# Where the attention values stand around a loop of routed expert tiles, and how scores are masked

## The chip, the cores and the metric

The kernel runs on one core of one Trainium2 chip. The metric is the device time of one execution in microseconds (us); all times below are in us unless a line says ns. Engines are named as in the profile: PE is TensorE (PEld its weight loads), DVE the vector engine, ACT ScalarE, POOL GpSimd, SP the engine that issues most DMAs.

## The reference, cut to what matters

Two layers over x of shape 2048 x 512, each of the form `x + attention(norm(x)) * silu(ffn(norm(x)))`. The change lies in the second layer:

```python
# attention: 28 pooled keys (means over 64 tokens) for the first 1792 tokens, the last 256 tokens as keys of their own
scores = (q_sem @ k_sem2.T + q_geo @ k_geo2.T) / sqrt(32) * exp(logit_scale)   # 16 heads
scores = where(k_pos <= pos, scores, -1e9)
s = (softmax(scores) @ v2) @ Wo
# mixture of experts: 2 shared experts, and the 4 best of 16 routed ones for each token
ffn = u + shared(u) + sum_over_chosen(gate * (relu(u @ w1 + b1) @ w2 + b2))
x = x + s * silu(ffn)
```

A token at position p sees the pooled keys of blocks that end at or before p. The first 63 tokens see none; for them the softmax over equal scores is uniform over all keys, local ones included.

## The kernel before, in words

All arithmetic is float32. The 2048 tokens are 16 attention tiles of 128 rows (`NT`). Tiles 14 and 15 (`FULL`) also see local keys and are done early, in `full_group`, beside shared-expert matmuls. Tiles 0 to 13 see pooled keys only: tile i uses the first (i+1)*2 of them (tile 0 uses all 32 columns, because of its rows that see nothing). `KP` is 32 columns for the pooled keys, `NARROW` is 16. For tiles with at most 16 keys the scores lie in a `near` buffer, else in a `wide` one (three of each, taken in turn).

The work on a pair of tiles ("block" b of 256 tokens, seven in all) has three sorts of parts:

- `queries` (L1352 to L1368): two parts, each a projection `pq` of 16 matmul records on TensorE and four vector operations, with loads of cosines and sines;
- `scores` (L1560 to L1572, then `softmax`, L1325 to L1335): one part per tile, eight plus eight matmul records into `ps`, a product with the mask `m_pool`, the addition of `n_pool`, maximum, subtraction, Exp on ScalarE, sum, reciprocal, product;
- `values` (L1585 to L1597): one part per tile, transposes `pt`, a ScalarE copy to `sT`, matmuls `pw` with the values that are already folded with Wo, and a ScalarE copy into `xT`, which then holds the attention output of that tile.

A masked score is made as `score * 0 + (-1e9)`, an open one as `score * 1 + 0`; `m_pool` and `n_pool` hold the factors and addends for all 16 tiles (`NT`) side by side, `m_full` and `n_full` those of the full tiles. They are built on POOL at L765 to L792, ahead of the gathers of `yg` (L832).

The routed experts are a list of up to 80 tiles of 128 rows (`NRT`), of which at least 64 (`FULL_TILES`) are in use. `hidden_rows(j)` loads the weights and rows of tile j, transposes the rows (`tp`, L1678), and makes the hidden rows (`ph`, L1685; `ht`, L942). `down_rows` (`py`, L1709; `y`, L1714) makes the outputs of the tile before and adds them to the sums `comb` in DRAM by two indirect DMAs on POOL's queue (L1717). From j = 65 on, each step is inside a conditional `tc.If(held > j - 1)` (L1749), whose content is a unit of its own. Attention parts are put between the routed tiles: 30 of the 42 parts are spread over the first 64 steps, and the last 12 behind the conditional steps (`LATE`, `parts_by`, `attend_by`). These twelve are the queries of blocks 5 and 6, the scores of tiles 10 to 13 and the values of tiles 10 to 13.

Behind the loop the kernel closes: for each of eight pairs of attention tiles it loads the sums from `comb` (L1777), applies Silu on ScalarE (L1783), multiplies by `xT` (L1785), adds the residual `xo` (L1789) and stores the result (L1790).

The framework's planner orders the instructions of each engine at build time. It goes by program order, but moves work ahead that it takes for ready while an engine would be idle. `tc.keep_in_program_order(ins)` ties an instruction behind the one traced before it on its engine in the same block of code.

Of the kernel before, what the change touches and what calls it, by code (L numbers as in the profile page):

```python
# [9 lines left out]
F32 = mybir.dt.float32  # L10
# [67 lines left out]
def tile_kernel(ctx: ExitStack, tc: tile.TileContext, a: dict):  # L78
# [656 lines left out]

    sm_sem = ak.tile([P, HKV, 4], F32, name="sm_sem")
    sm_geo = ak.tile([P, 2, 8], F32, name="sm_geo")
    m_pool = ak.tile([P, NT, KP], F32, name="m_pool")
    n_pool = ak.tile([P, NT, KP], F32, name="n_pool")
    wt_pool = ak.tile([P, KP], F32, name="wt_pool")  # L740
    oh = ak.tile([P, NRT, NR], F32, name="oh")
# [22 lines left out]

    nc.gpsimd.memset(m_pool, 1.0)  # L765
    nc.gpsimd.memset(n_pool, 0.0)
    for t_, fill in ((m_pool, 0.0), (n_pool, MASKED)):
        nc.gpsimd.affine_select(
            out=t_, in_=t_, compare_op=ALU.is_ge, fill=fill, base=1 - MB,
            pattern=[[P, NT], [-MB, KP]], channel_multiplier=1,  # L770
        )
    nc.gpsimd.memset(m_pool[:, :, NBLK:KP], 0.0)
    nc.gpsimd.memset(n_pool[:, :, NBLK:KP], PADDED)


# [2 lines left out]
    nc.gpsimd.memset(wt_pool[:, NBLK : NBLK + 1], float(LW))  # L778


    m_full = ak.tile([P, KA], F32, name="m_full")
    n_full = [ak.tile([P, KP + (u + 1) * P], F32, name=f"n_full{u}") for u in range(len(FULL))]
    nc.gpsimd.memset(m_full, 1.0)
    for u, i in enumerate(FULL):
        nc.gpsimd.memset(n_full[u], 0.0)
        nc.gpsimd.tensor_copy(n_full[u][:, 0:KP], n_pool[:, i, :])
    for t_, fill in ((m_full, 0.0), *((t_, MASKED) for t_ in n_full)):
        own = t_[:, t_.shape[1] - P :]
        nc.gpsimd.affine_select(
            out=own, in_=own, compare_op=ALU.is_ge, fill=fill, base=0,  # L790
            pattern=[[-1, P]], channel_multiplier=1,
        )  # L792

# [525 lines left out]
    aps = ctx.enter_context(tc.tile_pool(name="aps", bufs=3, space=PSUM))  # L1319
    QB = 256  # L1320

    def softmax(s, heads, keys, neg, wt=None, last=True):

        sh_ = [P, heads, keys]
        nc.vector.tensor_tensor(out=s, in0=s, in1=bc(neg, 1, sh_), op=ALU.add)  # L1325
        mx = small.tile([P, heads], F32, tag=f"mx{heads}", name="mx")
        nc.vector.tensor_reduce(out=mx, in_=s, axis=AX.X, op=ALU.max)
        nc.vector.tensor_tensor(out=s, in0=s, in1=bc(mx, 2, sh_), op=ALU.subtract)
        nc.scalar.activation(s, s, AF.Exp)
        if wt is not None:  # L1330
            nc.vector.tensor_tensor(out=s, in0=s, in1=bc(wt, 1, sh_), op=ALU.mult)
        nc.vector.tensor_reduce(out=mx, in_=s, axis=AX.X, op=ALU.add)
        nc.vector.reciprocal(out=mx, in_=mx)
        if last:
            nc.vector.tensor_tensor(out=s, in0=s, in1=bc(mx, 2, sh_), op=ALU.mult)  # L1335
        return mx
# [39 lines left out]
    with tc.tile_pool(name="fw", bufs=1, side="right") as fw:  # L1376
# [51 lines left out]
        def full_group(u, g, woa):  # L1428
# [6 lines left out]
            for h in range(4):  # L1435
                rr = slice(HP * (h % 2), HP * (h % 2) + HP)
                ps = aps.tile([P, KA], F32, tag="pa", name="ps")
                nc.tensor.matmul(
                    out=ps[:, 0:nk], lhsT=qf[rr, 2 * g + h // 2, cols], rhs=kf[rr, g, 0:nk],
                    start=True, stop=True,  # L1440
                )
                nc.vector.tensor_tensor(
                    out=s[:, h, :], in0=ps[:, 0:nk], in1=m_full[:, KA - nk :], op=ALU.mult
                )
            mx = softmax(s, 4, nk, n_full[u], last=False)
            sp = fw.tile([P, 4, KP], F32, tag="sp", bufs=2, name="sp")
            for out, ks in ((sp, slice(0, KP)), (s[:, :, KP:nk], slice(KP, nk))):
                nc.vector.tensor_tensor(
# [91 lines left out]

    wide = [aq.tile([P, H, KP], F32, name=f"wide{i}") for i in range(3)]
    near = [aq.tile([P, H, NARROW], F32, name=f"near{i}") for i in range(3)]
    for t_ in (*wide, *near):
        nc.gpsimd.memset(t_, 0.0)
# [1 line left out]
    def room_of(i):  # L1548

        if i == 0:  # L1550
            return aq.tile([P, H, KP], F32, tag="t1", name="all_keys"), KP
        nk = (i + 1) * P // MB
        return (near if nk <= NARROW else wide)[i % 3], nk

    def scores(i, qg, u):
        cols = slice(u * P, (u + 1) * P)
        room, nk = room_of(i)
        ps = aps.tile([P, H, nk], F32, tag="pa", name="ps")
        for c in range(NC):
            nc.tensor.matmul(  # L1560
                out=ps, lhsT=xT[:, c, i * P : (i + 1) * P], rhs=sem[:, c, :, 0:nk],
                start=(c == 0), stop=False,
            )
        for p in range(2):
            for hf in range(2):
                nc.tensor.matmul(
                    out=ps[:, 8 * p : 8 * p + 8, :], lhsT=qg[:, p, hf, cols],
                    rhs=kd_geo[:, hf, 8 * p : 8 * p + 8, 0:nk], start=False,
                    stop=(p == 1 and hf == 1),
                )  # L1570
        s = room[:, :, 0:nk]
        nc.vector.tensor_tensor(  # L1572
            out=s, in0=ps, in1=bc(m_pool[:, i, 0:nk], 1, [P, H, nk]), op=ALU.mult
        )
        softmax(s, H, nk, n_pool[:, i, 0:nk], wt_pool if i == 0 else None)
        return room

    def values(i, s):
        keys = s.shape[2]
        each = P // keys  # L1580
        by_row = vo if keys == KP else vo8
        nw = H // each
        pt = aps.tile([P, nw, P], F32, tag="pa", name="pt")
        for g in range(nw):
            nc.tensor.transpose(  # L1585
                pt[:, g, :], s[:, each * g : each * (g + 1), :].rearrange("p h k -> p (h k)"),
                ident,
            )
        sT = aq2.tile([P, HKV, P], F32, tag="sT", name="sT")
        nc.scalar.copy(sT[:, 0:nw, :], pt)  # L1590
        pw = aps.tile([P, NC, P], F32, tag="pa", name="pw")
        for g in range(nw):
            nc.tensor.matmul(  # L1593
                out=pw.rearrange("p c t -> p (c t)"), lhsT=sT[:, g, :], rhs=by_row[:, g, :],
                start=(g == 0), stop=(g == nw - 1),
            )
        nc.scalar.copy(xT[:, :, i * P : (i + 1) * P], pw)  # L1597

    def attention():


        nb = FULL[0] * P // QB
        n = QB // P
        got = {}

        def start(b):
            return queries(
                b, aq, lambda shape: [aq.tile(shape, F32, tag=t, name=t) for t in ("t1", "t2")]
            )

        def score(b, u, q):
            got[b * n + u] = scores(b * n + u, q[0], u)

        def value(i):
            values(i, got.pop(i))

        for b in range(nb - 1):
            q = start(b)
            yield from q[1]
            if b < nb - 2:  # L1620
                for u in range(n):
                    score(b, u, q)
                    yield
                for u in range(n):
                    value(b * n + u)
                    yield
        assert n == 2
        for u in range(n):
            score(nb - 2, u, q)
            yield  # L1630
        q = start(nb - 1)
        yield from q[1]
        value((nb - 2) * n)
        yield
        for u in range(n):
            score(nb - 1, u, q)
            yield
        for i in ((nb - 2) * n + 1, (nb - 1) * n, (nb - 1) * n + 1):
            value(i)
            yield  # L1640


    iop = m1f.tile([P, 1], I32, name="iop")
# [76 lines left out]
            )  # L1720

    FULL_TILES = T * KR // P
    MAYBE = NRT - FULL_TILES
    PARTS = 6 * (FULL[0] * P // QB)
    LATE = 12
    attend = attention()
    rest_of = {}
    held = nc.values_load(
# [1 line left out]
        skip_runtime_bounds_check_because="it is a sum of counts, FULL_TILES to NRT",  # L1730
    )

    def parts_by(j):

        if j < FULL_TILES:
            return (j + 1) * (PARTS - LATE) // FULL_TILES
        return PARTS - LATE + (j - FULL_TILES) * LATE // MAYBE

    pending, taken = None, 0

    def attend_by(j):
        nonlocal taken
        while taken < parts_by(j):
            next(attend)
            taken += 1

    for j in range(NRT + 1):

        with contextlib.ExitStack() as more:  # L1749
            if j > FULL_TILES:  # L1750
                more.enter_context(tc.If(held > j - 1))
            made = hidden_rows(j) if j < NRT else None
            if j <= FULL_TILES:
                attend_by(j)
            if pending is not None:
                down_rows(*pending)
            pending = (j, *made) if made is not None else None
# [1 line left out]
            if 0 <= i < NT and i % 2 == 0:  # L1759
# [2 lines left out]
                    out=xo, in_=xr1[i * P : (i + 2) * P, :].rearrange("(n p) d -> p n d", p=P)  # L1762
                )
                rest_of[i] = xo
        if j > FULL_TILES:
            attend_by(j)
    assert next(attend, None) is None

    tiles.close()
# [4 lines left out]
    for i in range(0, NT, 2):  # L1774
# [4 lines left out]
                in_=c_[i * P : (i + 2) * P, :].rearrange("(n p) d -> p n d", p=P),  # L1779
            )  # L1780
        sums_of[i] = y
    for i, y in sums_of.items():
        nc.scalar.activation(y, y, AF.Silu)  # L1783
        y4 = y.rearrange("p n (c t) -> p n c t", t=P)
        nc.vector.tensor_tensor(  # L1785
            out=y4, in0=xT[:, :, i * P : (i + 2) * P].rearrange("p c (n t) -> p n c t", t=P),
            in1=y4, op=ALU.mult,
        )
        nc.vector.tensor_tensor(out=y, in0=y, in1=rest_of[i], op=ALU.add)  # L1789
        nc.sync.dma_start(  # L1790
            out=a["out"][i * P : (i + 2) * P, :].rearrange("(n p) d -> p n d", p=P), in_=y
        )


# [91 lines left out]
```

## Time and profile before

| what | before |
|---|---|
| runs | 1944.71, 1953.96, 1950.14; median 1950.14 |
| profiled execution: time, span | 1940.83, 1939.1 |
| TensorE busy, granted clock | 96% of the span, 0.986 |
| DVE, ACT, POOL busy | 41%, 27%, 24% |
| routed tiles run in the profiled execution | 74 with hidden rows, 73 with outputs |
| TensorE's work on the last routed tile ends | 1862.2 |
| last indirect add is issued | 1873.2 |
| first load of `comb` is issued | 1881.5 |

The profiled execution is one of the faster ones: its time lies 9.3 below the median. A row of a timeline gives start, duration, engine, line, operation, output and inputs, shape and count; in brackets stands how long the engine was idle before it and what ended that. TensorE's matmuls in float32 are recorded as two instructions each.

### The profile page before, as it was taken

What the parts mean: (1) busy time and instruction counts of PE and PEld (TensorE: products, weight loads), DVE (VectorE), ACT (ScalarE), POOL (GpSimd) and SP (SyncE); (2) the same over time, 40 slices, a digit from 0 to 9 for tenths busy, and PEclk for the clock granted to TensorE, in tenths of its full rate; (3) what the DMA queues carried; (4) which work ended last, traced back from release to release, by engine and by line L of the source; (5) the groups of instructions that cost most, each with busy time, mean ns of one, the idle gap of its engine ahead of it and who ended that gap; (6) DMA issues with size and microseconds to landing.
All of it is one profiled execution on the core that took longest, in us unless ns stands there. A gap on an engine that the chain in (4) does not pass through costs nothing.

```text
span 1939.1 us, 23212 instructions
## 1 busy us (share of the span) xinstructions
PE 1857.2 (96%) x8107; PEld 1292.1 (67%) x8107; DVE 787.3 (41%) x1565; ACT 532.9 (27%) x994; POOL 465.9 (24%) x350
## 2 busy tenths in 40 slices
PE   5899999999999999999989999999999999999977
PEld 4677777787877777777533654444767777777654
DVE  8713627272634545252166544331323232223116
ACT  6212322232323232232134212221222222222223
POOL 1301212121201111020210453000344444444430
PEclk9799999999999999999999999999999999999998
DMA  7548685635654443436461553022999999999963
GB/s 250 205 144 278 205 306 178 221 108 163 197 195 141 130 131 125 157 98 233 147 227 46 174 215 114 31 95 87 313 290 316 320 311 298 292 282 265 299 148 131
DMA packets 214096, 381.35 MB, mean 197 GB/s; under 512 B 16972, under 2 KB 134476, under 8 KB 213080
## 3 DMA queue, kind: packets, MB, share of 16 engines
q1 hardware_dynamic: 183896, 332.78, 50.7%
q0 software_dynamic: 28784, 45.63, 10.7%
q10 hardware_dynamic: 1296, 1.41, 0.3%
q8 instruction: 67, 1.10, 0.2%
q14 instruction: 53, 0.43, 0.1%
HBM read 294.04 MB, written 85.72 MB: 196 GB/s over the span
## 4 chain that ended last, share of the span: by engine, by line
PE 83%; DMA 6%; DVE 3%; issue 2%; POOL 2%; ACT 2%; SPq 0%; POOLq 0%; ACTq 0%; DVEq 0%
PE pg L571 23%; PE py L593 12%; PE ph L1685 9%; PE py L1709 9%; PE proj L416 7%; PE py L1105 4%; PE ph L956 3%; PE pw L1593 2%; DMA comb<-y,to 2%; PE pq L1352 2%; PE tp L1678 1%; PE po L712 1%; PE ps L1560 1%; PE pl L870 1%; PE pw L1477 1%
## 5 line engine op out<-in xcount | busy, mean ns | idle before, releaser
L571 PE MATMUL pg<-xg,w 128*128 128x256 f32 (+1 forms) x2304 | 497.8, 369 | 3.3 <-ACT xg L563 3.3
L571 PEld LDWEIGHTS pg<-xg,w 128*128 128x128 f32 x2304 | 420.9, 191 | 95.0 <-issue 42.1
L1717 POOL DMA_INDIRECT comb<-y,to x146 | 226.9, 1554 | 300.0 <-DMA comb<-y,to 222.2
L593 PE MATMUL py<-wd,hT 128*128 128x512 f32 x544 | 256.9, 593 | 2.9 <-DVE hT L578 2.9
L1685 PEld LDWEIGHTS ph<-xg,w 128*128 128x128 f32 (+1 forms) x1776 | 201.9, 182 | 39.8 <-ACT xg L1680 32.9
L1685 PE MATMUL ph<-xg,w 128*128 128x128 f32 (+1 forms) x1776 | 214.4, 277 | 1.5 <-DMA w<-in_w_dram 1.5
L1709 PE MATMUL py<-w,ht 128*128 128x512 f32 (+1 forms) x438 | 209.1, 593 | 0.0
L578 DVE TENSOR_TENSOR hT<-sg,pg 128x256 f32<-128x256 f32 (+1 forms) x144 | 57.0, 402 | 338.4 <-ACT sg L576 338.3
L576 ACT ACTIVATE sg<-pg 128x256 f32<-128x256 f32 (+1 forms) x144 | 53.5, 372 | 419.7 <-PE pg L571 419.4
L593 PEld LDWEIGHTS py<-wd,hT 128*128 128x128 f32 x544 | 102.1, 190 | 72.2 <-issue 61.9
L1714 DVE TENSOR_SCALAR y<-py,g 128x512 f32<-128x512 f32 x73 | 54.6, 749 | 206.7 <-PE py L1709 196.1
L942 ACT ACTIVATE ht<-ph,b1t 128x128 f32<-128x128 f32 (+1 forms) x222 | 81.3, 366 | 178.9 <-PE ph L1685 161.4
L1709 PEld LDWEIGHTS py<-w,ht 128*128 128x128 f32 (+1 forms) x438 | 75.1, 191 | 49.8 <-issue 49.3
L1680 ACT COPY xg<-tp 128x512 f32<-128x512 f32 x74 | 43.4, 586 | 177.2 <-PE tp L1678 166.4
L1105 PE MATMUL py<-w,hT 128*128 128x512 f32 (+1 forms) x192 | 89.3, 596 | 0.0
L956 PE MATMUL ph<-xT,w 128*128 128x512 f32 (+1 forms) x192 | 88.0, 597 | 0.0
L1043 POOL DMA_INDIRECT xs<-acc,slot x64 | 63.1, 985 | 67.2 <-DMA xs<-acc,slot 43.5
L1352 PE MATMUL pq<-xT,wqg 128*128 128x256 f32 x224 | 56.6, 401 | 14.2 <-DVE wide L1572 9.6
L712 PE MATMUL po<-wo,yb 128*128 128x512 f32 x128 | 59.3, 620 | 9.6 <-ACT acc L721 5.5
L416 PE MATMUL proj<-xm,wr 128*128 128x256 f32 x256 | 60.9, 393 | 5.6 <-ACT v L452 5.6
L464 POOL TENSOR_TENSOR ex<-st_p,qt 128x1024 f32<-128x1024 f32 x8 | 18.3, 2288 | 193.0 <-DVE qt L463 193.0
L1678 PEld LDWEIGHTS tp<-ident,x 128*128 128x128 f32 x296 | 36.7, 140 | 38.8 <-issue 21.5
(418 smaller groups left out, 2180.9 us busy)
## 6 DMA issues: line engine op xcount, KB each, us to landing
w<-in_w_dram SPq DMA_DIRECT2D x76, 704.0 KB
w<-in_w_dram SPq DMA_DIRECT2D x76, 512.0 KB
w<-in_w_gate_dram SPq DMA_DIRECT2D x72, 512.0 KB
w<-in_w_up_dram SPq DMA_DIRECT2D x72, 512.0 KB
wd<-in_w_down_dram SPq DMA_DIRECT2D x72, 512.0 KB
xs<-zero SPq DMA_DIRECT2D x16, 1360.0 KB
x<-xs SPq DMA_DIRECT2D x74, 272.0 KB
w<-in_w_dram SPq DMA_DIRECT2D x76, 192.0 KB
```

The lines of the kernel that those rows point to most:

```text
L416: nc.tensor.matmul(out=ps[:, j, :], lhsT=w_[:, c, (o0 + j) * P : (o0 + j + 1) * P], rhs=xm[:, c, :], start=(c == 0), stop=(c == NC - 1),)
L571: nc.tensor.matmul(out=pg[:, i, 0:n], lhsT=w[:, c, i * FH + f * P : i * FH + (f + 1) * P], rhs=xg[:, c, 0:n], start=(c == 0), stop=(c == N ...
L593: nc.tensor.matmul(out=p, lhsT=hT[:, u * P : (u + 1) * P], rhs=wd[:, f, :], start=first_, stop=last_,)
L712: nc.tensor.matmul(out=po, lhsT=yb[:, c, s * P : (s + 1) * P], rhs=wo[:, c, :], start=(c == 0), stop=(c == NC - 1),)
L942: nc.scalar.activation(dst, src, AF.Relu, bias=b)
L956: nc.tensor.matmul(out=ph[0:n, :], lhsT=up(w, f, n, c), rhs=xT[:, c, cols], start=(c == 0), stop=(c == NC - 1),)
L1043: ins = nc.gpsimd.indirect_dma_start(out=xs, out_offset=bass.IndirectOffsetOnAxis(ap=slot[:, i, k : k + 1], axis=0), in_=acc[:, i, :], in_ ...
L1105: nc.tensor.matmul(out=py, lhsT=hT[0:n, e, f, s * P : (s + 1) * P], rhs=down(w, f, n), start=(e == 0 and f == 0), stop=(e == NS - 1 and f ...
L1352: nc.tensor.matmul(out=pq[:, j, :], lhsT=w[:, c, w0 : w0 + P], rhs=xT[:, c, tc0], start=(c == 0), stop=(c == NC - 1),)
L1685: nc.tensor.matmul(out=ph[0:n, :], lhsT=up(w, f, n, c), rhs=xg[:, c, :], start=(c == 0), stop=(c == NC - 1),)
L1709: nc.tensor.matmul(out=py, lhsT=hT[0:n, f, :], rhs=down(w, f, n), start=(f == 0), stop=(f == NF1 - 1),)
L1717: nc.gpsimd.indirect_dma_start(out=c_, out_offset=bass.IndirectOffsetOnAxis(ap=to, axis=0), in_=y[:, h * D // 2 : (h + 1) * D // 2], in_of ...
```

## The change

Three edits:

1. All queries and scores, and the values of tiles 0 to 7 (`WIDE` = 8), are parts of the loop: 36 parts spread evenly over the first 64 steps. The conditional steps hold no attention part between them.
2. The values of tiles 8 to 13 stand behind the last routed tile, in the closing: 8 to 11, then pairs 0 and 2, then 12, pairs 4 and 6, then 13, and the rest. Their first copies and all Silus are kept in program order on ScalarE. Tiles 8 to 13 have a `wide` buffer each (six in place of three).
3. Masks are one addition, `score + (-1e9)`, made while the scores leave PSUM. Only tile 0 still has the product, with an `m_pool` of one tile; `m_full` is gone.

```diff
-    m_pool = ak.tile([P, NT, KP], F32, name="m_pool")
+    m_pool = ak.tile([P, KP], F32, name="m_pool")
...
-    m_full = ak.tile([P, KA], F32, name="m_full")
-    nc.gpsimd.memset(m_full, 1.0)
...
-    for t_, fill in ((m_full, 0.0), *((t_, MASKED) for t_ in n_full)):
+    for t_ in n_full:
...
-        nc.vector.tensor_tensor(out=s, in0=s, in1=bc(neg, 1, sh_), op=ALU.add)
...
-                    out=s[:, h, :], in0=ps[:, 0:nk], in1=m_full[:, KA - nk :], op=ALU.mult
-                )
-            mx = softmax(s, 4, nk, n_full[u], last=False)
+                    out=s[:, h, :], in0=ps[:, 0:nk], in1=n_full[u], op=ALU.add
+                )
+            mx = softmax(s, 4, nk, last=False)
...
-    wide = [aq.tile([P, H, KP], F32, name=f"wide{i}") for i in range(3)]
+    WIDE = NARROW * MB // P
+    wide = [aq.tile([P, H, KP], F32, name=f"wide{i}") for i in range(WIDE, FULL[0])]
...
+        if i == 0:
+            nc.vector.tensor_tensor(out=s, in0=ps, in1=bc(m_pool, 1, sh_), op=ALU.mult)
+            ps = s
         nc.vector.tensor_tensor(
-            out=s, in0=ps, in1=bc(m_pool[:, i, 0:nk], 1, [P, H, nk]), op=ALU.mult
-        )
-        softmax(s, H, nk, n_pool[:, i, 0:nk], wt_pool if i == 0 else None)
+            out=s, in0=ps, in1=bc(n_pool[:, i, 0:nk], 1, sh_), op=ALU.add
+        )
+        softmax(s, H, nk, wt_pool if i == 0 else None)
...
-        nc.scalar.copy(sT[:, 0:nw, :], pt)
+        ins = nc.scalar.copy(sT[:, 0:nw, :], pt)
+        if pinned:
+            tc.keep_in_program_order(ins)
...
+        for b in range(nb):
+            q = queries(...)
             yield from q[1]
+            for i in range(b * n, b * n + n):
+                waiting[i] = scores(i, q[0], i - b * n)
+                yield
+            for i in range(b * n, b * n + n):
+                if i < WIDE:
+                    values(i, waiting.pop(i))
                     yield
...
-    PARTS = 6 * (FULL[0] * P // QB)
-    LATE = 12
+    PARTS = 4 * nb + WIDE
...
-            if j <= FULL_TILES:
-                attend_by(j)
+            if taken < PARTS and (j + 1) * PARTS // FULL_TILES > taken:
+                next(attend)
+                taken += 1
...
-        if j > FULL_TILES:
-            attend_by(j)
...
-    for i, y in sums_of.items():
-        nc.scalar.activation(y, y, AF.Silu)
+    def close(i):
+        y = sums_of[i]
+        tc.keep_in_program_order(nc.scalar.activation(y, y, AF.Silu))
...
+    for i in (8, 9, 10, 11):
+        values(i, waiting.pop(i), pinned=True)
+    for i in (0, 2):
+        close(i)
+    values(12, waiting.pop(12), pinned=True)
+    for i in (4, 6):
+        close(i)
+    values(13, waiting.pop(13), pinned=True)
+    for i in (8, 10, 14, 12):
+        close(i)
```

More of the change, by code (lines that the diff above doesn't have):

```diff
@@ L766, in tile_kernel @@
     nc.gpsimd.memset(n_pool, 0.0)
[L767 to L770, printed above, removed]
-        )
-    nc.gpsimd.memset(m_pool[:, :, NBLK:KP], 0.0)
+    nc.gpsimd.affine_select(
+        out=m_pool, in_=m_pool, compare_op=ALU.is_ge, fill=0.0, base=1 - MB,
+        pattern=[[-MB, KP]], channel_multiplier=1,
+    )
+    nc.gpsimd.affine_select(
+        out=n_pool, in_=n_pool, compare_op=ALU.is_ge, fill=MASKED, base=1 - MB,
+        pattern=[[P, NT], [-MB, KP]], channel_multiplier=1,
+    )
+    nc.gpsimd.memset(m_pool[:, NBLK:KP], 0.0)
     nc.gpsimd.memset(n_pool[:, :, NBLK:KP], PADDED)
@@ L786, in tile_kernel @@
         nc.gpsimd.tensor_copy(n_full[u][:, 0:KP], n_pool[:, i, :])
-    for t_, fill in ((m_full, 0.0), *((t_, MASKED) for t_ in n_full)):
+    for t_ in n_full:
         own = t_[:, t_.shape[1] - P :]
         nc.gpsimd.affine_select(
-            out=own, in_=own, compare_op=ALU.is_ge, fill=fill, base=0,
+            out=own, in_=own, compare_op=ALU.is_ge, fill=MASKED, base=0,
             pattern=[[-1, P]], channel_multiplier=1,
@@ L1320, in tile_kernel, with softmax @@
     QB = 256
-    def softmax(s, heads, keys, neg, wt=None, last=True):
+    def softmax(s, heads, keys, wt=None, last=True):
         sh_ = [P, heads, keys]
-        nc.vector.tensor_tensor(out=s, in0=s, in1=bc(neg, 1, sh_), op=ALU.add)
         mx = small.tile([P, heads], F32, tag=f"mx{heads}", name="mx")
@@ L1552, in room_of @@
         nk = (i + 1) * P // MB
-        return (near if nk <= NARROW else wide)[i % 3], nk
+        return (near[i % 3] if i < WIDE else wide[i - WIDE]), nk
     def scores(i, qg, u):
@@ L1571, in scores, with values @@
         s = room[:, :, 0:nk]
+        sh_ = [P, H, nk]
+        if i == 0:
+            nc.vector.tensor_tensor(out=s, in0=ps, in1=bc(m_pool, 1, sh_), op=ALU.mult)
+            ps = s
         nc.vector.tensor_tensor(
-            out=s, in0=ps, in1=bc(m_pool[:, i, 0:nk], 1, [P, H, nk]), op=ALU.mult
+            out=s, in0=ps, in1=bc(n_pool[:, i, 0:nk], 1, sh_), op=ALU.add
         )
-        softmax(s, H, nk, n_pool[:, i, 0:nk], wt_pool if i == 0 else None)
+        softmax(s, H, nk, wt_pool if i == 0 else None)
         return room
-    def values(i, s):
+    def values(i, s, pinned=False):
         keys = s.shape[2]
@@ L1597, in values @@
         nc.scalar.copy(xT[:, :, i * P : (i + 1) * P], pw)
+    nb = FULL[0] * P // QB
+    n = QB // P
+    waiting = {}
     def attention():
[L1602 to L1607, printed above, removed]
+        for b in range(nb):
+            q = queries(
                 b, aq, lambda shape: [aq.tile(shape, F32, tag=t, name=t) for t in ("t1", "t2")]
             )
[L1611 to L1618, printed above, removed]
-            yield from q[1]
-            if b < nb - 2:
-                for u in range(n):
-                    score(b, u, q)
-                    yield
[L1624 to L1640, printed above, removed]
+            yield from q[1]
+            for i in range(b * n, b * n + n):
[4 more added lines that the diff above has]
+                    values(i, waiting.pop(i))
+                    yield
     iop = m1f.tile([P, 1], I32, name="iop")
@@ L1722, in tile_kernel @@
     FULL_TILES = T * KR // P
-    MAYBE = NRT - FULL_TILES
-    PARTS = 6 * (FULL[0] * P // QB)
-    LATE = 12
+    PARTS = 4 * nb + WIDE
     attend = attention()
@@ L1731, in tile_kernel @@
     )
[L1733 to L1737, printed above, removed]
     pending, taken = None, 0
[L1741 to L1745, printed above, removed]
     for j in range(NRT + 1):
@@ L1792, in tile_kernel @@
         )
+    for i in (8, 9, 10, 11):
[8 more added lines that the diff above has]
+        close(i)
+    assert not waiting
 def _arrays(inp):
```

## The prediction

> **What bounds the kernel now.** I read part 1 of the page first, then the windows by stage, then TensorE's timeline in the routed loop, then the timelines of all engines behind the last routed tile.
>
> ```profile
> PE 1857.2 (96%) x8107; PEld 1292.1 (67%) x8107; DVE 787.3 (41%) x1565; ACT 532.9 (27%) x994; POOL 465.9 (24%) x350
> ```
>
> ```profile
> 1500.00:1600.00 100.00, 100.00 (x573) 72.56 (x572) 29.47 (x101) 27.17 (x65) 41.46 (x27) 1.00 1.04 317
> ...
> 1880.00:1900.00 20.00, 8.67 (x28) 6.58 (x26) 10.85 (x17) 11.42 (x11) 0.00 (x0) 0.74 0.82 276
> 1900.00:1939.00 39.00, 28.27 (x80) 14.85 (x80) 24.29 (x36) 11.17 (x16) 0.00 (x0) 0.86 0.21 81
> ```
>
> (Columns: length, busy PE, PEld, DVE, ACT, POOL, granted clock, DMA share, GB/s.) In the loop TensorE is never idle; behind it everything is half idle and the clock drops. Is a full TensorE row the bound, or only modelled? The distance between the input transposes (tp) of successive tiles tells:
>
> ```profile
> 1740.10 0.60 PE L1678 MATMUL tp<-ident,x 128*128 128x128 f32 x4
> 1745.91 0.60 PE L1678 MATMUL tp<-ident,x 128*128 128x128 f32 x4
> 1754.54 0.60 PE L1678 MATMUL tp<-ident,x 128*128 128x128 f32 x4
> 1760.35 0.60 PE L1678 MATMUL tp<-ident,x 128*128 128x128 f32 x4
> 1769.27 0.60 PE L1678 MATMUL tp<-ident,x 128*128 128x128 f32 x4
> ...
> 1805.82 4.05 PE L1352 MATMUL pq<-xT,wqg 128*128 128x256 f32 x18
> ...
> 1866.81 4.73 PE L1352 MATMUL pq<-xT,wqg 128*128 128x256 f32 x14 [4.65 <-PEq L1749]
> ...
> 1892.00 6.23 PE L1352 MATMUL pq<-xT,wqg 128*128 128x256 f32 x16 [9.56 <-DVE wide L1572]
> 1900.82 1.08 PE L1585 MATMUL pt<-ident,wide 128*128 128x128 f32 x4 [2.59 <-DVE wide L1335]
> 1902.58 6.05 PE L1593 MATMUL pw<-vo,sT 128*128 128x512 f32 x8 [0.67 <-ACT sT L1590]
> ...
> 1923.38 3.70 PE L1593 MATMUL pw<-vo,sT 128*128 128x512 f32 x8 [0.73 <-ACT sT L1590]
> ```
>
> A bare tile takes 5.81; with the scores of attention tile 8 (288 columns) 8.63, of tile 9 (320) 8.92. What is put into the loop lengthens it by its own TensorE time. Behind the last tile (TensorE's work on it ends at 1862.2) stand three query projections, four scores, four values. They stall on the vector engine's order, and ScalarE changes tables for them:
>
> ```profile
> 1886.77 1.28 ACT L1783 ACT_TABLE_LOAD   x1 [24.15 <-DMA y<-comb]
> 1888.07 2.95 ACT L1783 ACTIVATE y<-y 128x1024 f32<-128x1024 f32 x3
> ```
>
> ```profile
> 1889.15 2.36 DVE L1785 TENSOR_TENSOR y<-xT,y 128x1024 f32<-128x1024 f32 x2 [15.46 <-ACT y L1783]
> 1891.43 0.52 DVE L1572 TENSOR_TENSOR wide<-ps,m_pool 128x352 f32<-128x352 f32 x1
> ...
> 1933.87 1.23 DVE L1789 TENSOR_TENSOR y<-y,xo 128x1024 f32<-128x1024 f32 x1
> ```
>
> Scores of tiles 10 and 11 lay ready in PSUM while the vector engine waited 15.46 for a closing product in front of them. The last sum ends at 1935.1; the span ends 4.0 later.
>
> **The change part by part.** Frame: the profiled execution, span 1939.1, time 1940.83. That is 0.5% under the median of the runs shown, 1950.14; I carry the difference over.
>
> *Into the loop.* One projection and 2 of the 16 matmuls of the next stood there already (the x18 row), so 2.88 projections enter. One costs 3.45 (tp at 1444.77 and 1454.03: 9.26 less 5.81): 9.9. Scores of tiles 10 to 13: 2.82 and 3.11 for tiles 8 and 9, so 0.29 a step: 3.40 + 3.69 + 3.98 + 4.27 = 15.3. Values 8 and 9 leave: tp at 1790.45 and 1800.00 give 9.55, so 3.74 each, -7.5. Sum **+17.7**, all on the path. Their softmaxes (5 to 6 operations of about 0.6) lie beside the matmuls, DVE being 29% busy there; without that cover some 14. The cosine and sine loads move from SP's queue behind the loop (0.47 + 0.43 of issue, between loads of comb) to among the weight loads, one more SP stop of that length twice; weights are three deep, so nothing.
>
> *Values 8 to 13.* The order in code isn't the order on an engine: the x18 row was traced between conditional tiles and ran ahead of the first of them, about 3.9 of work. The pin ties an instruction only to the one traced before it on ScalarE, so a value can slip into that gap too. I take one (value 8): +3.74 and 0.7 for its copy = +4.4 (ends: none, 0; four, 17.6). The others start behind the skipped conditionals (1866.8), one each 4.87 (the rows at 1918.52 and 1923.38), the first of them 2.4 slower: 9 to 11 end near 1884. The sums in comb are not loaded before 1886.77, so the first Silu stays at **1888.07**.
>
> *The closing.* From that Silu on, ScalarE runs in program order, and the Silu of pair 4 stands behind the copy of value 12, which waits for its matmuls. Two Silus 2.12, sT 0.63, pw, xT 0.65, two Silus 2.12, sT 0.6, pw, xT 0.65, Silu 1.06, then the vector engine's last four pairs 4 x 2.46 = 9.84, and 4.0 to the end. What does pw take? The trace has 3.70 after an idle 0.73, and 6.05 after idles of 9.56 and 2.59. Before values 12 and 13 TensorE now idles about 8 and 3.4. The Trainium skill, "TensorE: Matmul & The Clock Gate", section "Why this matters for your kernels", speaks against the change: after a pause of about 3 us the clock falls back to half. With 3.70 twice the closing takes 29.1, with 6.05 twice 33.8; by rule and rows I take 33.8. End 1888.07 + 33.8 = 1921.9, against 1939.1: **-17.2**.
>
> *Table loads.* Six of 1.28 stand behind the loop before, one will: the Exps go where Relu and copies cause none (the trace shows none in the loop). "ScalarE: Activation LUTs", section "Rules for kernel authors", budgets about 2.7 a switch; my sum holds one, so that figure would add 1.4. I keep the row's.
>
> *Masks.* On POOL they stand ahead of the gathers yg, on the chain that ended last:
>
> ```profile
> 956.13 0.73 POOL m_pool L768
> ...
> 957.68 0.27 POOL m_full L783
> ...
> 959.79 1.03 POOL yg L832
> ```
>
> m_pool shrinks to a sixteenth (memset 0.46 to about 0.06, select 0.73 to about 0.28), m_full goes (0.27 and 0.25): **-1.4**. In the full tiles 8 additions go (4 x 0.83, 4 x 1.36 = 8.7 of DVE), but TensorE fills that time with shared-expert rows (19.68 to 20.00 busy of each 20.00): 0, at most the 0.7 that it idles there; without that cover it would be a gain of 8.7. Thirteen products in the scores (0.23 to 0.62) also lie beside the loop: 0. Three more wide buffers cost POOL 1.5 near 1294, where it next waits 2.53 for TensorE: 0, or 1.5 without that wait.
>
> *Sum:* 17.7 + 4.4 - 17.2 - 1.4 = **+3.5**: work is moved from a badly ordered tail into a loop that has no room. 1940.83 becomes 1944.3, the median 1953.6.
>
> **The rivals.**
> *B, slower: the pins do not hold the values back.* The planner pulls several of values 8 to 11 ahead of the first conditional tile. Each costs 3.74 + 0.7 in a full loop and gains nothing, because the first Silu waits for comb at 1886.77 anyway. It decides from the third value on (+12.3); with four +16.8: 1967. For it: the x18 row. Against: that gap held only 3.9.
> *C, faster: ScalarE's order costs nothing.* Values 12 and 13 hide behind the vector engine, which then closes without a hole: 1888.07 + 1.06 + 8 x 2.46 + 4.0 = 1912.8, -26.3; with no value pulled ahead 17.7 - 26.3 - 1.4 = -10.0: 1940. For it: pw at 3.70 in a warm stretch. Against: Silu and copies are in one queue.
> *D: the loop has room.* DMA share is 1.04 there; if transfers set the pace, the added matmuls are free: -17.2 - 1.4 = -18.6: 1931.5. Against: the 5.81 and its increments.
>
> **How the numbers follow.** Half a per cent (9.75) is about what a measurement of this kernel can tell from no change. The main case has 0.55: no value to two pulled ahead, pw warm or cold, -4 to +8, with the spread of medians (runs from 1944.71 to 1953.96) 1944 to 1961 by itself. B 0.25, C 0.14, D 0.06. Faster: half of C, D, 0.01 of the main case: 0.14. Slower: 0.22 of B, 0.09 of the main case: 0.31. The range leaves out D, C's far half and the top of B: 1942 to 1969.
>
> **What would show it.** Right: in the changed profile tp distances stay 5.81 plus the part's own time; the last routed tile ends 16 to 22 later; one table load behind it; the first Silu about 26 after TensorE's last routed work; two holes of 3 to 7 in DVE's closing, each ended by a Silu; pw of values 12 and 13 near 6; the gathers 1.4 earlier. Wrong: several pw between the last full tile and the first conditional one (B), closing products without holes (C), or a loop that is no longer (D). A changed order ahead of 950 would be something that I do not foresee.

## The result, and the profile after

| | before | changed |
|---|---|---|
| median of 13 runs each | 1945.79 | 1934.14 |
| lowest to highest | 1938.61 to 1957.56 | 1930.03 to 1944.87 |
| profiled execution: time, span | 1940.83, 1939.1 | 1930.89, 1929.2 |

The ratio is 0.9945, 95% interval 0.9927 to 0.9963: 0.55% faster. The forecast was 1953.6, with 1942 to 1969 as its range, and leaned to slower. Time and sign were missed.

Read the changed profile in the order of the prediction: part 1 of the page and the windows first, then TensorE's timeline, ScalarE, the vector engine.

```profile
PE 1849.7 (96%) x8107; PEld 1286.6 (67%) x8107; DVE 772.0 (40%) x1544; ACT 525.4 (27%) x989; POOL 467.0 (24%) x351
```

```profile
1500.00:1600.00 100.00, 100.00 (x573) 74.54 (x572) 28.55 (x92) 25.42 (x61) 41.93 (x28) 1.00 1.00 299
1880.00:1900.00 20.00, 14.54 (x40) 6.88 (x40) 0.00 (x0) 5.80 (x9) 4.65 (x3) 0.91 0.52 116
1900.00:1929.00 29.00, 9.54 (x20) 3.96 (x20) 18.44 (x16) 9.22 (x12) 0.00 (x0) 0.72 0.64 228
```

The loop is as full as before. From its last routed work to the end TensorE has 24.1 of work in place of 50.1. Its timeline, the transposes and multiplications of the values:

```profile
1821.04 0.60 PE L1590 MATMUL pt<-ident,wide 128*128 128x128 f32 x4
1822.31 3.70 PE L1600 MATMUL pw<-vo,sT 128*128 128x512 f32 x8 [0.67 <-ACT sT L1595]
1881.22 0.63 PE L1590 MATMUL pt<-ident,wide 128*128 128x128 f32 x4 [2.91 <-PEq L1717]
1882.53 5.20 PE L1600 MATMUL pw<-vo,sT 128*128 128x512 f32 x8 [0.67 <-ACT sT L1595]
...
1901.93 5.40 PE L1600 MATMUL pw<-vo,sT 128*128 128x512 f32 x8 [4.03 <-ACT sT L1595]
1907.16 0.60 PE L1590 MATMUL pt<-ident,wide 128*128 128x128 f32 x4
1910.38 3.70 PE L1600 MATMUL pw<-vo,sT 128*128 128x512 f32 x8 [2.61 <-ACT sT L1595]
```

Exactly one value (tile 8, at 1821.04) ran ahead of the conditional tiles, as forecast. Values 9 to 11 follow at 1881.22. ScalarE:

```profile
1897.51 0.59 ACT L1604 COPY xT<-pw 128x512 f32<-128x512 f32 x1 [3.79 <-PE pw L1600]
1898.11 1.28 ACT L1752 ACT_TABLE_LOAD   x1
1899.40 2.00 ACT L1752 ACTIVATE y<-y 128x1024 f32<-128x1024 f32 x2
```

One table load, as forecast, directly behind the copy of value 11. No idle time stands in front of it, where before had 24.15 for the loads of `comb`: the first Silu now follows that copy, and the sums are no longer what it waits for. The vector engine, and the only two pauses in its closing (the first row's label names the loads, but its Silu had begun only at 1899.40):

```profile
1900.49 2.36 DVE L1754 TENSOR_TENSOR y<-xT,y 128x1024 f32<-128x1024 f32 x2 [24.18 <-DMA y<-comb]
...
1908.94 2.36 DVE L1754 TENSOR_TENSOR y<-xT,y 128x1024 f32<-128x1024 f32 x2 [3.81 <-ACT y L1752]
...
1915.69 2.36 DVE L1754 TENSOR_TENSOR y<-xT,y 128x1024 f32<-128x1024 f32 x2 [2.12 <-ACT y L1752]
```

The span is cut into stages by instructions that both traces have (starts: the first `po` behind the 940 mark, the first gather `yg`, the first `tp` of the loop, the last hidden rows `ph`, the first Silu):

| stage | before | changed | difference | forecast |
|---|---|---|---|---|
| start to that `po` | 951.97 | 948.33 | -3.6 | 0 |
| to the first gather `yg` | 7.82 | 6.31 | -1.5 | -1.4 |
| to the first `tp` | 390.51 | 388.53 | -2.0 | 0 |
| to the last `ph` | 508.94 | 532.22 | +23.3 | +22.1 |
| to the first Silu | 28.83 | 24.01 | -4.8 | 0 |
| to the end | 51.03 | 29.80 | -21.2 | -17.2 |
| sum | | | -9.9 | +3.5 |

The miss between the two profiles is 13.4. The first and third rows (5.6 together) are within the spread of executions, as the runs below show; the fifth holds 4.8, and the sixth is 4.0 beyond its forecast. The fifth is the one that matters: behind the last tile the sums were ready sooner, and the values of tiles 8 to 11 fill the wait for them. What follows tests why.

### The profile page after: what moved, and what is told of

It is laid out like the page before. It is cut to its first block, busy times and chain, and to the rows that moved or that the text cites. A ratio compares the mean times of both kernels' runs of the same rounds, so it can differ in the third digit from the quotient of the medians.

```text
span 1929.2 us, 23186 instructions
## 1 busy us (share of the span) xinstructions
PE 1849.7 (96%) x8107; PEld 1286.6 (67%) x8107; DVE 772.0 (40%) x1544; ACT 525.4 (27%) x989; POOL 467.0 (24%) x351
## 3 DMA queue, kind: packets, MB, share of 16 engines
q0 software_dynamic: 28784, 45.63, 10.8%
## 5 line engine op out<-in xcount | busy, mean ns | idle before, releaser
L545 POOL DMA_INDIRECT xr<-in_x_dram,tok x17 | 23.2, 1365 | 160.4 <-PE tp L560 133.2
```

## Twelve experiments

### Each half of the edit alone

The kernel before with the masks alone (`score + n_pool` on leaving PSUM, small `m_pool`, no `m_full`):

> The kernel before with the mask edit alone (one addition, one-tile m_pool, no m_full); all 42 attention parts stand as before. Theory (prediction's term): only POOL's memsets and selects ahead of the gathers get shorter, -1.4, everything behind moves by the same: about 0.1% faster, first routed hidden matmul 1.5 earlier. Rival: the edit also changes the planner's order between 950 and 1340 (two POOL instructions and eight additions less), and that gives the further 2.2 by which the changed kernel reached the routed loop sooner: -3.7 by the first routed hidden matmul, about 0.2% faster. Second rival: the four or so microseconds that the changed kernel has gained by 951 belong to the edit too: then -7.

Measured: 1947.87, ratio 1.0000 (0.9982 to 1.0018). From `po` to `yg` are 6.31 where before has 7.82, so the -1.4 was right to 0.1. It can't be seen in the time: 1.4 is 0.07%, and the interval reaches 0.18% to each side. The profiled execution also lost more behind the masks than they gained: TensorE waited once, 4.41, for `xg` (ScalarE's copy of a tile's transposed rows) in the loop, and the first Silu came 32.8 behind the last hidden rows. The further 2.2 of the first rival do not show: from `yg` to the first `tp` are 390.0 here, 390.5 and 388.4 in two profiles of before. Nor does the second: `po` started at 947.9 to 952.4 in the profiles of this study, at 948.66 with the masks of before (the longer rings below).

The changed kernel with the old product in the pooled scores:

```diff
-    m_pool = ak.tile([P, KP], F32, name="m_pool")
+    m_pool = ak.tile([P, NT, KP], F32, name="m_pool")
...
-            out=s, in0=ps, in1=bc(n_pool[:, i, 0:nk], 1, sh_), op=ALU.add
+            out=s, in0=ps, in1=bc(m_pool[:, i, 0:nk], 1, [P, H, nk]), op=ALU.mult
+        )
+        nc.vector.tensor_tensor(
+            out=s, in0=s, in1=bc(n_pool[:, i, 0:nk], 1, [P, H, nk]), op=ALU.add
```

> The changed kernel with the product and addition masks of before in the pooled tiles (the 16-tile m_pool and 13 products are back; the full tiles keep one addition, since six wide buffers and m_full do not fit in memory together). Theory: the order of parts gives what the two traces show behind the first routed hidden matmul: loop +22, closing -27.5 (first Silu 21 instead of 26 behind TensorE's last routed work, then 30 to the end instead of 51), so -4 to -6 against before, 0.2 to 0.3% faster, and 3 to 4 slower than the changed kernel. Rival (the prediction's sum): +4.9 without the masks' -1.4, 0.25% slower. Rival 2: DVE's products in the loop cost nothing and the whole gain is the order: 0.5% faster.

Measured: 1936.37, ratio 0.9955 (0.9937 to 0.9974). The order makes the gain. The theory's 0.2 to 0.3% lies at the edge of the interval (0.26 to 0.63%); the last rival's 0.5% lies inside it. The stages are near those of the changed kernel: loop 531.1, first Silu 26.0 behind the last hidden rows, closing 31.3.

### Where the values stand

All fourteen values in the loop:

```diff
-                if i < WIDE:
-                    values(i, waiting.pop(i))
-                    yield
+                values(i, waiting.pop(i))
+                yield
...
-    PARTS = 4 * nb + WIDE
+    PARTS = 6 * nb
...
+    for i in range(0, NT, 2):
+        close(i)
```

> The changed kernel with the values of tiles 8 to 13 in the loop as well; behind the last routed tile only Silu, product, sum and store of eight pairs. Theory: each value costs its own 3.74 of TensorE in the loop; one of the six was there already, so five more are 18.7 (less the 0.7 copy of value 8); the first Silu then waits for comb alone, about 20 behind TensorE's last routed work (1 sooner at most), and DVE closes without holes, 1.06 + 8 x 2.46 + 4.0 = 24.7 in place of 29.8: +18.7 - 1 - 5.1 = +12.6 against the changed kernel, 0.65% slower than it and about 0.1% slower than before. Rival: the loop has slack for values (weights or the scatter adds set the pace): then -6, 0.3% faster than the changed kernel.

Measured: 1950.28, ratio 1.0022 (1.0003 to 1.0040), so 0.8% slower than the changed kernel. The loop (first `tp` to last `ph`) took 549.2, 16.9 more, and the closing 23.6 without a hole. The loop has no room: rival D of the prediction falls. But the first Silu came 28.7 behind the last hidden rows, not under 24, and it waited 24.00 for the loads of `comb`: a longer loop alone doesn't make the sums ready sooner. The table below comes back to this.

Without the pins:

```diff
-        if pinned:
-            tc.keep_in_program_order(ins)
...
-        tc.keep_in_program_order(nc.scalar.activation(y, y, AF.Silu))
+        nc.scalar.activation(y, y, AF.Silu)
```

> The changed kernel without keep_in_program_order on the copies sT and on the Silus; TensorE's order is the same. ScalarE's order is now value 8, first copy of value 9, Silu, the rest of value 9, copy of 10, four Silus, value 10, and so on. Theory: the Silu waits for comb until about 1898, so values 9 to 13 start 15 later and run between the Silus: four values of 4.9 to 6 each behind 1899 with the last at about 1930, plus product, sum and store 6.5: end about 1936, +7 against the changed kernel, about even with before. Rival: the vector engine has eight pairs to close (19.7) anyhow and the values hide behind them: 0.

Measured: 1934.29, ratio 0.9948 (0.9929 to 0.9966), the same as the changed kernel. The rival holds: values 9 to 13 ran between and behind the Silus, the last copy at 1924.25, and from first Silu to end were 29.6. Here the first Silu waited for the sums (13.99) and still came 24.0 behind the last hidden rows. Program order on ScalarE isn't what brings the gain.

### The queue of adds behind the loop

Each routed tile ends in two indirect adds to `comb`, and the comb loads of the closing wait for the last of them. In the views of what the vector engine waits for (columns: who, for whom, us in total, times, longest), from 1340 to 1900, first before, then changed:

```profile
DVE to L1703 <- DMA comb<-y,to: 101.5, 30, 6.7
```

```profile
DVE to L1686 <- DMA comb<-y,to: 6.1, 5, 3.0
```

`to` holds the row addresses of an add. It has six buffers, so this wait means that the add of six tiles before, counted by the making of the addresses, still holds its buffer. To see whether that was luck, both kernels were profiled a second time, unchanged.

> The kernel before once more, for a second profile of it: its profiled execution took 1940.8 where its runs have a median near 1947. Theory: between executions the backlog of indirect adds at the end of the loop differs (in the first profile the second add of the last tile was issued 13.1 behind the end of the multiplication that makes its rows); here it is 14 to 19 and the first Silu comes 29 to 33 behind the start of the last hidden rows, as in the kernel with the masks alone (14.7, 32.8). Rival: the executions differ ahead of the loop, and the stretch from the last hidden rows to the first Silu is 28.8 again.

> The changed kernel once more, for a second profile and to stand beside the two others of this call. Theory: DVE's wait for an indirect add in front of the addresses to stays under 10 in all (6.1 in the first profile; 101.5 to 139 with the old order), no wait of TensorE for a copy xg in the loop, the last add is issued 9 to 14 behind the start of the last hidden rows; ratio to before about 0.9945. Rival: the short queue of adds in the first profile was luck, and the wait and the 14 to 21 of the old order are seen here as well.

Measured: before 1951.67 (one run), changed 1934.85, ratio 0.9954 (0.9937 to 0.9971). Before again, its waits and two places in TensorE's timeline:

```profile
DVE to L1703 <- DMA comb<-y,to: 161.0, 40, 7.3
...
DVE y L1714 <- DMA comb<-y,to: 32.8, 6, 7.6
```

```profile
1665.85 4.33 PE L1685 MATMUL ph<-xg,w 128*128 128x128 f32 x24 [3.07 <-ACT xg L1680]
...
1854.61 1.95 PE L1709 MATMUL py<-w,ht 128*128 128x512 f32 x4 [1.16 <-ACT ht L942]
```

The vector engine stands still for a free `to` or a free `y`, and TensorE now and then waits for ScalarE. In this profile the first Silu came at 1898.50, 35.0 behind the last hidden rows. In the changed kernel's second profile the wait for `to` was 37.0 (more than the 10 expected, a third to a quarter of before), no `xg` was waited for, and the first Silu came 24.0 behind, as in the first.

The lag of a tile is the time from the end of the product `y` to the issue of its second add; tiles are counted from 0, and the last is 72.

| profile | wait for `to` | lag at tile 62 | lag at the last tile | last add behind last `ph` | first Silu behind last `ph` |
|---|---|---|---|---|---|
| before, shown | 101.5 | 10.3 | 13.1 | 14.0 | 28.8 |
| before again | 161.0 | 15.8 | 13.1 | 21.0 | 35.0 |
| before with the masks | 139.2 | 11.7 | 14.7 | 18.9 | 32.8 |
| changed | 6.1 | 2.5 | 8.1 | 9.0 | 24.0 |
| changed again | 37.0 | 2.5 | 8.6 | 9.5 | 24.0 |
| all values in the loop | none | 2.1 | 13.9 | 14.8 | 28.7 |

Up to tile 62, where attention parts stand between the tiles, the new order lets the adds catch up and the old one doesn't. From tile 64 on the tiles are bare in all of them, and the queue fills again: to 12.1 in the changed kernel, to 18.0 in before, but to 17.3 with all the values in the loop, although that loop is the longest and its queue was as good as empty. (In before again the last `y` itself came 7 later.)

Now half of the adds are taken away, in both kernels alike:

```diff
-        for h, c_ in enumerate(comb):
+        for h, c_ in enumerate(comb[:1]):
             nc.gpsimd.indirect_dma_start(
```

> The kernel before with one indirect add for each routed tile in place of two (the upper 256 columns of the routed sums are left out). Theory: the adds run behind the loop because two of them take nearly as long as a bare tile of 5.81; with one the lag of the last tile falls from 13.1 (14.7 in the kernel with the masks alone) to 2 or 3, the first Silu comes about 10 sooner, DVE's 15.46 in front of the closing product shrinks by as much, and the kernel is 9 to 13 faster than before: 0.5 to 0.65%. Rival: the adds are off the path, since DVE and TensorE have enough to do behind the loop: under 3 faster.

> The changed kernel with one indirect add for each routed tile in place of two (the upper 256 columns of the routed sums are left out). Theory: its lag at the end is 8.1 and falls to 2 or 3, but the first Silu stands behind the copy of value 11, which ended at 1898.1 against 1898.11 for the table load; so only 0 to 2 are gained, and the difference to the kernel before with one add shrinks from 11 or so to within 3: the change's gain was a shorter queue of adds. Rival: the gain has other causes, and the difference with one add is still about 10.

Measured: the old order 1934.00, ratio 0.9939 (0.9915 to 0.9963); the new one 1939.57, ratio 0.9951 (0.9930 to 0.9972). With one add the advantage of the new order is gone; by the medians it is 5.6 behind, by the intervals no difference shows, and the prediction's +3.5 lies within them. The first product of the old order's closing shows where most of its 12 came from; in the profile of before the same row read 15.46 and 1889.15:

```profile
1880.51 2.36 DVE L1785 TENSOR_TENSOR y<-xT,y 128x1024 f32<-128x1024 f32 x2 [8.74 <-DMA y<-comb]
```

The new order gains nothing from the second add's absence. Its loads of `comb` are issued at 1889.1 in place of 1892.7, but the table load again follows the copy of value 11 without idle time, and the first Silu came 25.8 behind the last hidden rows:

```profile
1898.91 0.59 ACT L1604 COPY xT<-pw 128x512 f32<-128x512 f32 x1 [3.79 <-PE pw L1600]
1899.52 1.28 ACT L1752 ACT_TABLE_LOAD   x1
```

Does the backlog cost by holding the vector engine, or by making the sums late? Longer rings take most of the first away:

```diff
-        to = m1x.tile([P, 1], I32, tag="to", bufs=6, name="to")
+        to = m1x.tile([P, 1], I32, tag="to", bufs=16, name="to")
...
-        y = m1x.tile([P, D], F32, tag="y", bufs=4, name="y")
+        y = m1x.tile([P, D], F32, tag="y", bufs=6, name="y")
```

> The kernel before with 16 buffers in place of 6 for the addresses to and 6 in place of 4 for the rows y; TensorE's order is unchanged. Theory: the backlog of adds costs in two ways; DVE waits for a free to (101.5 in one profile), holds up softmax and thereby ScalarE and now and then TensorE (3.1 to 4.4 each time); and the sums come late at the end. This edit takes the first away only: DVE's wait for to falls to 0, no wait of TensorE for xg, while the backlog itself stays (last add 14 to 21 behind the start of the last hidden rows): 0 to 5 faster than before. Rival 1: the whole loss of the old order comes from the held-up DVE: 9 to 13 faster. Rival 2: nothing, since TensorE's stalls have another cause.

Measured: 1949.31, ratio 1.0017 (1.0002 to 1.0033): not faster. No wait for `to` is left and no wait of TensorE for `xg`; waits for a free `y` are, 24.3 in all. The rows came at 7.08 a tile (tiles 12 to 63), as in the shown profile of before. But the backlog grew: the lag was 11 at tile 13, 20 at tile 21, 30 at tile 36 and 38.7 at tile 65. So the full ring had been a brake on the backlog. TensorE paid nothing for it in the shown profile of before, where the adds took 7.01 a tile in the same stretch; how the brake helps the adds was not tried. The bill came at the end, on ScalarE, 43.0 behind the last hidden rows:

```profile
1900.93 1.28 ACT L1783 ACT_TABLE_LOAD   x1 [38.34 <-DMA y<-comb]
1902.22 2.05 ACT L1783 ACTIVATE y<-y 128x1024 f32<-128x1024 f32 x2
```

With these rings the adds took 7.56 a tile (tiles 12 to 63), and 4.56 a tile over the last five, when no weights came in any more. That points at the DMA engines. Last run: the longer rings, and weights loaded for three tiles only, then used again in turn (the routed outputs are those of three sets of weights).

```diff
+            kept.append(w)
...
-            w = weights()
+            w = kept[j % FIRST]
```

> The kernel with the longer rings, with one further thing left out: the routed weights are loaded for the first three tiles only and used again in turn by all others (the routed outputs are those of three sets of weights). TensorE's work is the same, the loop's DMA traffic nearly gone. Theory: the adds are slow because they share the DMA engines with the weights: with the longer rings they took 7.56 a tile in the loop (rows came at 7.08) and 4.54 a tile once the weights were in; here they take what the rows take, the lag stays at 2 to 5 throughout instead of growing to 37, and the last add is issued 5 to 9 behind the start of the last hidden rows. About 15 faster than before. Rival: two adds one behind the other take 7.5 by themselves: the lag grows to 30 or more again.

Measured: 1927.94, ratio 0.9884 (0.9846 to 0.9922). The lag of the second add is 2.1 to 2.4 at nearly every tile from the seventh on, and 2.1 at the last. The last add is issued 3.1 behind the last hidden rows, the first Silu 16.6. The windows of the loop, with the weights and without (DMA share and GB/s at the end):

```profile
1400.00:1800.00 400.00, 400.00 (x2268) 289.43 (x2267) 110.63 (x376) 107.55 (x255) 164.95 (x107) 1.00 0.99 294
```

```profile
1400.00:1800.00 400.00, 400.00 (x2272) 289.79 (x2270) 110.31 (x376) 107.62 (x256) 175.69 (x113) 1.00 0.47 80
```

TensorE is 100% busy in both. Only the second kernel has room on the DMA engines, and there the adds keep up with the same work. The old order is then faster than the changed kernel with all its weights. So the adds compete with the weight loads, and TensorE's row can't show that. Whether they meet in the DMA engines or in the memory behind them isn't separated here.

### Two attempts at a better closing

Silus first, values 12 and 13 between them, their second copies last:

```diff
+    for i, v in ((0, 12), (2, 13), (4, None), (6, None), (8, None), (10, None), (14, None)):
+        silu(i)
+        close(i)
+        if v is not None:
+            made[v] = values(v, waiting.pop(v), pinned=True, later=True)
+    for i, pw in made.items():
+        tc.keep_in_program_order(nc.scalar.copy(xT[:, :, i * P : (i + 1) * P], pw))
+    silu(12)
+    close(12)
```

> The changed kernel with another order on ScalarE in the closing: Silu of pair 0, first copy of value 12, Silu of pair 2, first copy of value 13, five Silus, then the second copies of values 12 and 13, then the Silu of pair 12, which alone needs them. Theory: the two holes of the changed kernel's closing (3.81 and 2.12 idle of DVE in front of products that waited for a Silu) go: end = first Silu + 1.06 + 8 x 2.4 + 4.0, about 24.5 in place of 29.8: 5 faster than the changed kernel, 0.8% faster than before. Rival: DVE's products slow down or the stores at the end set the time: 0 to 2 faster.

Measured: 1935.69, ratio 0.9944 (0.9924 to 0.9965), no gain. The expectation overlooked TensorE's order: the transposes of value 13 stand behind the multiplications of value 12, so the copy pinned ahead of five Silus waited 4.75 and the vector engine paused for 3.48. Beside that the last add came 13.9 behind the last hidden rows.

Then value 12 ahead of the first Silu, so that TensorE doesn't pause, and a one-column Silu at the front for the table:

```diff
+    tc.keep_in_program_order(nc.scalar.activation(early, early, AF.Silu))
     for i in (8, 9, 10, 11):
         values(i, waiting.pop(i), pinned=True)
+    made = {12: values(12, waiting.pop(12), pinned=True, later=True)}
+    for i in (0, 2, 4):
+        close(i)
+    made[13] = values(13, waiting.pop(13), pinned=True, later=True)
+    for i in (6, 8, 10, 14):
+        close(i)
```

> The changed kernel with (1) a one-column Silu right behind the conditional tiles, so that the table load (1.28) stands before the sums come, (2) the first copy of value 12 ahead of the first Silu, so that TensorE goes from value 11 to value 12 without a pause, (3) that of value 13 behind three Silus and the second copies of values 12 and 13 behind the Silu of pair 14. Its pin also keeps the multiplications of value 8 behind the conditional tiles. Theory: the multiplications of value 12 take 3.70 in place of 5.40, DVE's closing has no hole above 1, and from the first Silu to the end are 24.5 in place of 29.8; with the table load 1.3: 5 to 7 faster than the changed kernel, 0.8% faster than before. Rival: the stores or the loads of comb set the closing's pace: under 2.

Measured: 1931.84, ratio 0.9931 (0.9911 to 0.9950); the changed kernel beside it had 0.9954 (0.9937 to 0.9971). It is the fastest full version, but the intervals overlap. The multiplications of value 12 took 3.70, and from the first Silu to the end were 25.4 in place of 29.8. Most of that was given back: the last add came 17.2 behind the last hidden rows, and the first Silu 29.5. What made the adds late here was not tried by itself; the last weights were issued 6.3 ahead of the last hidden rows (7.3 with all the values in the loop), in the changed kernel 10.4.

## Why the prediction was wrong, point by point

**The failed step** is the one behind "The sums in comb are not loaded before 1886.77, so the first Silu stays at **1888.07**": the 26 between TensorE's last routed work and the first Silu were taken for a property of the closing. They are the tail of a queue, the adds to `comb`, to which the prediction gave no term. In the old order the rows came at 7.08 to 7.20 a tile (tiles 12 to 63), and the adds took 7.01 to 7.56 while weights load, so a lag of 10 to 36 stood at tile 62. In the new order the rows come at 7.45, and the lag there is 2.5. So a part of the time that the attention work adds to the loop is time that the adds needed anyway, and it is gained back behind the loop. With the first Silu counted from the last hidden rows this is -4.8 in the two profiles compared, and -11.0 against the second profile of before. In this order it could hardly be more: the prediction had the values of tiles 8 to 11 end some 3 ahead of the sums, and now the Silu waits for them. That the queue is what the new order gains on is shown by the kernels with one add, where both orders take about the same time. That the longer loop is why the queue is shorter at the end is shown up to tile 62 only: with all the values in the loop the last bare tiles filled it to a tail of 28.7 again.

**The base was off, too.** "I carry the difference over" treated the 9.3 between the profiled execution and the median of three runs as belonging to any kernel. Over 13 runs the median of before is 1945.79, so 4.35 of the 9.3 were the chance of three runs. The changed kernel's profiled execution lies 3.25 below its median. Together this accounts for 6.1 of the 19.5 by which the median was missed; the other 13.4 are in the stage table. The queue is one cause of the spread: the second profile of before, 10.8 longer than the first, had 6.0 of that in the loop (3.6 of it TensorE's waits for `xg`) and 6.1 between the last hidden rows and the first Silu, less small gains elsewhere. The shown profile was an execution with a shorter backlog.

**The closing** was mis-sized by 4.0 (33.8 forecast, 29.8 measured). The multiplications were taken at 6.05 twice; they took 5.40 and 3.70, which is 3.0. The rest is small rows, two Silus in 2.00 in place of 2.12 among them. The mechanism was right: two holes, each ended by a Silu, though of 3.81 and 2.12 where 3 to 7 were forecast.

**Right** were the price of the loop (+23.3 against +22.1; 23.9 between the kernels with one add, but 17.2 against the second profile of before, whose loop had waits), the one value pulled ahead, one table load in place of six, and the masks at POOL (-1.5). That the loop costs its full TensorE time holds with all the values in it, too: five more were put at 18.7, and 16.9 were measured.

**Ahead of 951** the code is the same, and the 3.6 there is the spread of executions; the 2.0 to the first `tp` lie within it as well.

**The rivals.** B did not happen. C's difference of -10.0 met the -9.9 of the profiles by luck: its reason, a closing without holes, is wrong. D's 1931.5 lies nearest to the measured median, also by luck. It said that transfers set the pace and the loop has room; the loop has none, but transfers did set the pace of something else, the adds, which no case of the prediction had.

Left open: how far the last bare tiles fill the queue, and so why the lag at the last tile differs among kernels that all had 2.1 to 3.5 at tile 62 (8.1 in the changed kernel, 13.0 with the split values, 13.9 with all the values in the loop, 15.2 with the warm closing).

## What to carry to other kernels

When a resource is 96% busy, look also for a queue behind it that is nearly as full: for each consumer, compare the rate at which it is fed with the rate at which it drains, and follow its lag from tile to tile. Work put into a full loop then costs its time once, but may shorten a tail that waits for that queue (it did in the changed kernel, and not with all the values in the loop); and a ring that is always full may be a brake whose release only moves the wait to the end. A profile that is faster than the median may be the one with the short queue; profile twice before carrying its difference to another kernel.

## What the runs showed of the hardware that was not expected

- With the longer rings, two indirect adds of 128 rows x 256 columns took 7.56 per tile at a DMA share of 0.99 and 4.56 per tile after the weight loads had ended. POOL's own part is 1.55 each in both.
- From the issue of the last add to the issue of the first load of `comb` passed 8.1 to 8.4 in every profile.
- Eight `pw` took 3.70 after a pause of 0.73, always. After 2.61 they took 3.70 in the changed kernel (granted clock 1.00) and 5.13 with one add; after 2.53, 5.26 with the warm closing (0.70); after 4.03, 5.40 in the changed kernel (0.69) and 6.47 with one add. The Trainium skill, "TensorE: Matmul & The Clock Gate", section "Why this matters for your kernels", gives a pause of about 3 us for the fall of the clock. The 4.03 agree with it; 5.13 and 5.26 after shorter pauses do not, so the length of the last pause alone doesn't tell which it will be.
- The skipped conditional tiles held TensorE for 2.9 (changed) to 5.3 (longer rings), with the same steps left out.
